# Eleven of 49 convolution taps on ScalarE and adding DMAs, and a folded layernorm inside fc1

## The chip, the cores and the metric

The kernel runs on one core of a Trainium2 chip. The metric is the device time of one execution in microseconds (us). The kernel before was timed three times: 3348.62, 3349.13 and 3350.71 us; the median is 3349.13. The profile is of one more execution, of 3348.34 us, whose span from the first to the last instruction is 3346.6 us. Engines are called as in the profile: PE (matmuls; PEld is its weight load), DVE (vector), ACT (scalar), POOL (GpSimd) and SP (the queue that issues most DMAs).

## The reference

Everything is float32. The input `x` has 8 images of 384 channels and 32 x 32 points. Two layers follow each other.

```python
# layer 0: attention block on 1024 tokens of 384 channels, per image
xn  = layernorm(xf, g1, beta1)
qkv = xn @ w_qkv.T + b_qkv                      # 8 heads of 48
out = softmax(q k^T * 48**-0.5) v
x1  = out @ w_proj.T + b_proj + xf
h   = gelu(layernorm(x1, g2, beta2) @ w_fc1.T + b_fc1)   # 384 -> 1536
x   = x1 + h @ w_fc2.T + b_fc2
# layer 1: convolution block
y   = depthwise_conv7x7(x, dw_w, padding=3) + dw_b
y   = layernorm(y over channels) * ln_w + ln_b
y   = gelu(y @ w1 + b1)                         # 384 -> 1536
y   = grn_gamma * (y * nx) + grn_beta + y       # nx from the norms of y over the image
x   = x + y @ w2 + b2
```

Each layernorm takes, for every token, the mean and the variance over the 384 channels.

## The kernel before

Channels lie on the 128 partitions, so an image is a tile of 128 x 3 x 1024; "half" h is a run of 512 tokens[...]. Both layers are done for one image after the other, and two images are in work at once: while PE does attention and mlp of image b, DVE does the 7 x 7 convolution of image b-1 and afterwards PE does the second layer of image b-1.

The program writes the order of every engine's work by hand. PE's matmuls are written in sequence; each helper that issues them tells `Flow.pe` how long they take (U = 0.857 us for one 128 x 128 by 512 product). Work of the other engines is written as generators, "chains": each yields the time after which its next step is due, and `Flow` takes that step as soon as the clock of PE's work has passed it. A chain spawned with `paced=True` counts its times from when a step was due, others from when it was taken. `flow.finish` issues all that is left of a chain at once. A due time only sets where an instruction stands in its engine's queue; what it has to wait for on the chip is set by semaphores. Every engine works its queue in order.

In the loop over images an iteration b from 1 to 6 runs: `qk` (queries and keys), `attention`, `mlp`, `keep` (the result goes to DRAM for later), `grn_up` of image b-1, `start_conv(b)`, `next_values(b+1)`, `grn_down` of image b-1. Image 7 has its own, `mlp_by_halves` and a convolution in pieces.

**Attention** has 64 steps; a step computes scores (four matmuls into a bank pair of `ps_s`, of which there are two), an exp of 128 x 1024 on ACT (`L601`), and two steps later the product with the values. When a head pair is complete, `average` divides by the softmax sums: a copy on ACT, an addition on DVE, and three short DMA hops on SP's queue. After step 38 `proj` of half 0 is put between, and ln2 of half 0 is spawned; `rest` does the second half, and is called inside fc1.

**mlp**: fc1 takes 12 tiles of half 0, with `rest` and ln2 of half 1 after the fourth, then 12 tiles of half 1, each with a Gelu on ACT. Then `before_fc2` is called, and fc2 follows as 15 products of a fast 3 x 3 x 2 scheme (`by_thirds`), with many additions on DVE and some as adding DMAs on POOL (`L786`). `grn_down` (w2) uses the same scheme.

**The convolution** (`convolution`, `L897`) has 49 taps for each of three channel tiles: one DVE instruction of 128 x 1024 each, the padded image times a column of weights plus the accumulator `acc`. Its paces `us` are 1.6 for image 0, 1.8 or 1.5 later, the first 30 instructions at 2.43. `next_norms`, called before fc2, finishes it.

**Layernorm** (`layernorm`): DVE adds the three channel tiles, a matmul with ones gives the sum over partitions (`token_sums`), DVE subtracts the mean, ACT squares, and the same is done for the variance; ACT makes the inverse root by Ln and Exp (which needs a table load[...]), and DVE multiplies. `token_sums` has a straight form, one 128 x 128 matmul for each half (`L374`), and a folded one: an adding DMA of POOL (`L382`) puts one half of the partitions on the other, 3.4 us are left for it, and 64 x 64 matmuls follow (`L388`), those of two halves in different quadrants of the array. `abreast` runs both halves side by side, with its times multiplied by a factor (1.4). ln1 and the first half of ln2 are folded; ln3, the convolution's layernorm, is not, and is spawned in `next_norms`, so it runs during fc2. `block_differences` prepares four combinations of its result.

`grn_scale` makes the factors of the second layer's norm and multiplies the 12 tiles of y by them on ACT (`L1074`). Tiles named "res" come from a ring of three.

Of the kernel before, what the change touches and what calls it, by code (L numbers as in the profile page):

```python
# [46 lines left out]
F32 = mybir.dt.float32  # L47
# [18 lines left out]
NC = HT // CM  # L66
U = 0.857
SCALE = HD ** -0.5
EPS0, EPS1, GRN_EPS = 1e-5, 1e-6, 1e-6
# [81 lines left out]
def block_kernel(  # L151
# [24 lines left out]
    ps_o = ctx.enter_context(tc.tile_pool(name="ps_o", bufs=4, space=PSUM))  # L176
    flow = Flow()
    s_fc2 = dram.tile([P, len(FORMS), 4 * P], F32, tag="s_fc2", bufs=1, name="s_fc2")
    s_w2 = dram.tile([P, len(FORMS), 4 * P], F32, tag="s_w2", bufs=1, name="s_w2")
# [186 lines left out]

    def token_sums(t, name, fold):

        width = t.shape[-1]
        if fold is None:
            total = o_tile(name)[:, :width]
            nc.tensor.matmul(out=total, lhsT=ones, rhs=t, start=True, stop=True)  # L374
            flow.pe(U * width / NH)
            return [(total, slice(0, width))]
        rows = [slice(0, 64), slice(64, P)]
        parts = [(fold, slice(0, width))]
        if fold == "columns":
            parts = [(j, slice(j * width // 2, (j + 1) * width // 2)) for j in range(2)]  # L380
        for j, cols in parts:
            nc.gpsimd.dma_start(out=t[rows[j], cols], in_=t[rows[1 - j], cols], accum_op=ALU.add)  # L382
        yield 3.4
        totals = []
        for j, cols in parts:
            total = o_tile(f"{name}_{j}")[:, : cols.stop - cols.start]
            for i in rows:
                nc.tensor.matmul(out=total[i, :], lhsT=ones[rows[j], :64], rhs=t[rows[j], cols], start=True, stop=True)  # L388
            flow.pe(U * width / NH / 2)
            totals.append((total, cols))  # L390
        return totals

    def layernorm(src, dst, h, eps, g, name, switch, spare=None, spaced=False, slow=1.0, fold=None, gentle=False):

# [15 lines left out]
        yield 2.6 * slow  # L410
        totals = yield from token_sums(a, f"{name}_sum{h}", fold)
        yield 0.8
# [18 lines left out]
        yield 1.8 * slow  # L431
        totals = yield from token_sums(squares[0], f"{name}_var{h}", fold)
        yield 0.8
# [21 lines left out]

    def abreast(*args, places=averages, fold=True, gentle=False, factor=1.4):

        chains = [
            layernorm(*args[:2], h, *args[2:], spare=places if h else None, fold=h if fold else None, gentle=gentle)
            for h in range(2)  # L460
        ]
        while chains:
            waits = []
            for chain in list(chains):
                wait = next(chain, None)
                if wait is None:
                    chains.remove(chain)
                else:
                    waits.append(wait)
            if waits:  # L470
                yield factor * max(waits)
# [109 lines left out]
    def attention(b, xt, qT, kT, last_tile, first):  # L581
# [44 lines left out]
        for n in range(len(steps) + 2):  # L626
# [4 lines left out]
            if n >= 2:  # L631
                product(*steps[n - 2], ps.pop(n - 2))
            if n - 2 == len(steps) // 2 + 6:
                for chain in first:
# [4 lines left out]
                proj(b, xt, 0)  # L639
                slow = 1.4 if b in (1, B - 1) else 1.0  # L640
                ln = layernorm(xt, xn, 0, eps0, "g2", f"ln2_{b}", False, spaced=True, slow=slow, fold="columns")
                ln = flow.spawn(ln)

        def rest():
            for m in (NP - 1, *range(CT)):
                flow.finish(chains[1, m])
            for seen, op in ((low, ALU.min), (high, ALU.max)):
                ext = small.tile([P, 1], F32, tag="ext", name=f"ext_{b}_{op.name}")
                nc.vector.tensor_reduce(ext, sums, AX.X, op)
                nc.vector.tensor_tensor(seen, seen, ext, op)  # L650
            proj(b, xt, 1)

        return ln, rest, xn
# [63 lines left out]

    def mlp(b, xt, xn, weights, tag, ln, rest, before_fc2):

# [4 lines left out]
        for m in range(HT):  # L724
            gelu_half(hid, m, 0, xn, weights, wa, f"fc1_{b}")
            if m == 3 and rest:
                rest()
                slow = 1.2 if b == 1 else 1.0
                ln = flow.spawn(layernorm(xt, xn, 1, eps0, "g2", f"ln2_{b}", True, slow=slow))
        flow.finish(ln)  # L730
        for m in range(HT):
# [147 lines left out]

    def convolution(acc, us, slow=0, y0=0, y1=H, ready=tuple(range(CT))):  # L880

# [3 lines left out]
        ct, n = None, 0  # L885
        while min(done) < KS * KS:
            left = [c for c in ready if done[c] < KS * KS]
            ct = min([c for c in left if c != ct] or left, key=lambda c: done[c])
# [10 lines left out]
            n += 1  # L899
            yield 2.43 if n <= CT * slow else us  # L900

    def block_differences(acc):
# [77 lines left out]
    def grn_down_straight(b, y, kept, weights, tag, index, todo):  # L980
# [5 lines left out]
        def load():  # L986
            if len(res) < len(todo):
                r, part = todo[len(res)]
                t = three.tile([P, NH], F32, tag="res", name=f"res_{b}_{r}_{part.start}")[:, : part.stop - part.start]
                nc.sync.dma_start(out=t, in_=kept[r * P : (r + 1) * P, part])  # L990
# [164 lines left out]
    def prepare(weights, aside):  # L1155
# [25 lines left out]
        def spare(name):  # L1181
            return three.tile([P, NH], F32, tag="res", name=name)

# [121 lines left out]
    def main():  # L1305
# [40 lines left out]

        state = {"xn": xn, "conv": None, "acc": None, "norm1": None, "norm3": None}
        kept = {}

        def start_conv(b, us, slow=0):  # L1350
            state["acc"] = one.tile([P, CT, N], F32, tag="acc", name=f"acc_{b}")
            state["conv"] = flow.spawn(convolution(state["acc"], us, slow), paced=True)

        def next_norms(b, ln=None):

            if b > 0:
                acc = state["acc"]
                flow.finish(state["conv"])
                norm = abreast(acc, acc, eps1, "lnw", f"ln3_{b - 1}", True, fold=False)
                norm = sequence(norm, block_differences(acc)) if b < B - 1 else after(ln, norm)  # L1360
                state["norm3"] = flow.spawn(norm)
            if b + 1 < B:
# [21 lines left out]
        def last_convolution(h, ct, ln=None):  # L1384
            if ct < 0:
                next_norms(B - 1, ln)
                return
# [8 lines left out]
        for b in range(B):  # L1396
# [6 lines left out]
            if b < B - 1:  # L1403
                mlp(b, xt, xn, weights, b, ln2, rest, lambda: next_norms(b))
            else:
# [5 lines left out]
            if b == 0:  # L1411
                xt = load_x(b + 1, "x")
                flow.finish(preparing)
                start_conv(b, 1.6)
                next_values(1)
# [4 lines left out]
            if b < B - 1:  # L1420
                y, gx = grn_up(b - 1, acc, weights, b - 1)
                start_conv(b, 1.5 if b == B - 2 else 1.8, 10)
                scale = flow.spawn(grn_scale(b - 1, gx, weights, b - 1, y))
                next_values(b + 1)
                flow.finish(scale)
                grn_down(b - 1, y, xt, weights, b - 1, b - 1)
                xt = load_x(b + 1, "x")
            else:
# [34 lines left out]
    def exact_path():  # L1463

        load_wqkv(nc.scalar, nc.scalar)
        with tc.For_i(0, B) as b:
# [10 lines left out]
            ln = layernorm(xt, xn, 1, eps0, "g2", "ln2_x", True)  # L1477
            mlp("x", xt, xn, weights, "x", ln, None, None)
            kept = keep("x", xt)
# [110 lines left out]
```

## Time and profile before

| what | value |
|---|---|
| span | 3346.6 us |
| PE busy | 3303.6 us, 99% |
| DVE busy | 2550.6 us, 76% |
| ACT busy | 1421.0 us, 42% |
| POOL busy | 208.1 us, 6% |
| convolution taps of 128 x 1024 on DVE | 1008 of 1276 ns |
| exps of attention on ACT | 512 of 1024 ns |
| images 2 to 6 | 404.2 us each |

Busy time is what an engine's own instructions take; matmuls overlap, so a record of 592 ns can start 429 ns after the one before it, and a float32 matmul has two records. A line such as `L382` is a line of the kernel, which may be that of a helper. In a group of the profile, `out<-in` names the tiles, "xN" counts, and what follows "idle before" is how long the engine stood still before these instructions, and who released it. PEclk is PE's granted clock.

### The profile page before, as it was taken

How to read it: one execution, taken by the hardware profiler on the slowest of the kernel's cores; microseconds unless marked ns; L12 is line 12 of the kernel's file. 1: busy time of each engine (PE TensorE's matmuls, PEld its weight loads, DVE VectorE, ACT ScalarE, POOL GpSimd, SP SyncE). 2: the span in 40 equal slices, each digit the busy share in tenths (PEclk: the TensorE clock that was granted, in tenths of full speed). 3: DMA queues.
4: the chain of work that ended last, by engine and by line, in shares of the span. 5: the costliest groups of instructions: out<-in, count | busy, mean ns of one | idle time of the engine just before them, and what ended most of it. 6: DMA issues, size and time to landing. Idle time of an engine off the chain costs nothing.

```text
span 3346.6 us, 37477 instructions
## 1 busy us (share of the span) xinstructions
PE 3303.6 (99%) x14282; PEld 1416.7 (42%) x14282; DVE 2550.6 (76%) x3133; ACT 1421.0 (42%) x1884; POOL 208.1 (6%) x243
## 2 busy tenths in 40 slices
PE   8999999999999999999999999999999999999999
PEld 4344434443344433444334443444434444334455
DVE  4344788887877878779797796967888779989950
ACT  3442453444534354352552625426254353522641
POOL 2121000100000000100001000010000110000000
PEclk9999999999999999999999999999999999999999
DMA  5336102642125410445005350062501633023231
GB/s 185 111 105 148 52 20 57 158 102 63 25 70 146 115 47 20 105 122 135 20 16 131 96 140 17 17 157 80 128 18 37 170 83 95 20 56 90 62 98 50
DMA packets 151243, 281.59 MB, mean 84 GB/s; under 512 B 35216, under 2 KB 41232, under 8 KB 150672
## 3 DMA queue, kind: packets, MB, share of 16 engines
q1 hardware_dynamic: 114704, 201.32, 19.6%
q0 software_dynamic: 36064, 77.08, 11.9%
q8 instruction: 115, 1.88, 0.2%
q10 hardware_dynamic: 288, 0.71, 0.1%
q14 instruction: 72, 0.59, 0.1%
HBM read 181.52 MB, written 33.82 MB: 64 GB/s over the span
## 4 chain that ended last, share of the span: by engine, by line
PE 87%; DVE 10%; DMA 2%; issue 1%; ACT 0%; SPq 0%; POOL 0%; DVEq 0%; POOLq 0%
PE o L612 12%; PE s L592 12%; PE fc L345 12%; PE h L352 10%; PE fc_p L352 10%; PE o_p L352 9%; PE qk L332 6%; DVE wqkv L897 4%; PE v L521 4%; PE o L1000 4%; PE proj L535 3%; DVE acc L897 3%; PE h_last L1044 1%; PE qk_last L345 1%; PE ln_var L374 1%
## 5 line engine op out<-in xcount | busy, mean ns | idle before, releaser
L897 DVE SCALAR_TENSOR_TENSOR acc<-pad,vec,acc 128x1024 f32<-128x1024 f32 x1008 | 1230.6, 1276 | 0.0
L601 ACT ACTIVATE p<-s 128x1024 f32<-128x1024 f32 x512 | 523.6, 1024 | 380.6 <-PE s L592 378.4
L592 PE MATMUL s<-qk 48*64 48x512 f32 x4096 | 544.0, 592 | 1.6 <-ACT qk L495 1.5
L612 PE MATMUL o<-p,v 64*64 64x512 f32 x4096 | 538.9, 590 | 0.0
L345 PE MATMUL fc<-xn,fc 128*128 128x512 f32 x1152 | 500.4, 593 | 0.0
L345 PEld LDWEIGHTS fc<-xn,fc 128*128 128x128 f32 x1152 | 218.2, 190 | 278.2 <-issue 268.2
L352 PE MATMUL fc_p<-hid,fc 128*128 128x512 f32 x728 | 318.1, 592 | 0.0
L364 ACT ACTIVATE hid<-fc,bfc_f 128x512 f32<-128x512 f32 x192 | 130.9, 687 | 357.5 <-PE fc L345 357.4
L612 PEld LDWEIGHTS o<-p,v 64*64 64x64 f32 x4096 | 158.6, 133 | 284.6 <-issue 278.1
L592 PEld LDWEIGHTS s<-qk 48*64 48x64 f32 x4096 | 155.5, 133 | 286.0 <-issue 264.3
L945 DVE TENSOR_TENSOR y<-h,y 128x512 f32<-128x512 f32 x288 | 197.2, 690 | 97.8 <-PE h L352 87.3
L352 PE MATMUL o_p<-y,w 128*128 128x512 f32 x624 | 270.9, 592 | 0.0
L352 PEld LDWEIGHTS fc_p<-hid,fc 128*128 128x128 f32 x728 | 138.2, 190 | 174.4 <-issue 170.4
L332 PE MATMUL qk<-xn,wqkv 128*128 128x512 f32 x480 | 207.4, 592 | 0.0
L352 PE MATMUL h<-acc,w_A 128*128 128x512 f32 x432 | 206.4, 596 | 0.0
L897 DVE SCALAR_TENSOR_TENSOR wqkv<-pad,vec,wqkv 128x416 f32<-128x416 f32 (+1 forms) x288 | 193.7, 749 | 0.6
L352 PEld LDWEIGHTS o_p<-y,w 128*128 128x128 f32 x624 | 118.0, 190 | 148.7 <-issue 133.5
L553 DVE TENSOR_TENSOR attn<-o,attn 128x512 f32<-128x512 f32 x64 | 44.1, 689 | 147.2 <-ACT attn L551 147.2
L495 ACT ACTIVATE qk<-qk,bqk 128x1024 f32<-128x1024 f32 x40 | 44.6, 1114 | 229.0 <-PE qk L332 229.0
L712 ACT COPY pad<-x 128x512 f32<-128x512 f32 x48 | 30.2, 635 | 258.3 <-DVE x L777 192.4
L332 PEld LDWEIGHTS qk<-xn,wqkv 128*128 128x128 f32 x480 | 91.1, 190 | 114.1 <-issue 112.0
L535 PE MATMUL proj<-attn,wproj_sb 128*128 128x512 f32 x288 | 129.2, 602 | 2.1 <-DVE attn L579 2.1
(296 smaller groups left out, 3342.5 us busy)
## 6 DMA issues: line engine op xcount, KB each, us to landing
w_A<-in_w SPq DMA_DIRECT2D x72, 384.0 KB, 3.2
fc<-s_fc SPq DMA_DIRECT2D x91, 256.0 KB, 2.8
hid<-hid POOLq DMA_DIRECT2D x42, 512.0 KB, 6.7
fc<-in_wfc SPq DMA_DIRECT2D x54, 384.0 KB, 5.7
w<-s_w SPq DMA_DIRECT2D x78, 256.0 KB, 2.7
y<-y POOLq DMA_DIRECT2D x36, 512.0 KB, 7.0
kept<-x SPq DMA_DIRECT2D x8, 1536.0 KB, 8.3
xn<-in_x SPq DMA_DIRECT2D x14, 768.0 KB, 7.0
```

What stands on the lines that cost most here:

```text
L332: nc.tensor.matmul(out=ps[:, half(h)], lhsT=lhsT(k), rhs=rhs(k)[:, half(h)], start=(k == 0), stop=(k == nk - 1),)
L345: nc.tensor.matmul(out=ps, lhsT=lhsT(k), rhs=rhs(k)[:, half(h)], start=(k == 0), stop=(k == nk - 1))
L352: nc.tensor.matmul(out=bank, lhsT=lhsT, rhs=rhs, start=k == 0, stop=k == len(pairs) - 1)
L364: nc.scalar.activation(dst, src, function, **kw)
L521: nc.tensor.matmul(out=ps[:, :C], lhsT=xn[:, k, t * P : (t + 1) * P], rhs=wv_sb[:, k, :], start=(k == 0), stop=(k == CT - 1),)
L535: nc.tensor.matmul(out=ps, lhsT=wproj_sb[:, m, ct * P : (ct + 1) * P], rhs=attn[:, m, :], start=(m == 0), stop=(m == CT - 1),)
L592: nc.tensor.matmul(out=s[64 * i : 64 * i + 64, j, :], lhsT=kT[64 * j : 64 * j + HD, m, k0 : k0 + 64], rhs=qT[64 * j : 64 * j + HD, m, half ...
L601: nc.scalar.activation(p, s, AF.Exp)
L612: nc.tensor.matmul(out=outs[i][64 * j : 64 * j + 64, :], lhsT=v[keys, t, at : at + 64], rhs=p[keys, j, :], start=(t == 0), stop=(t == KT - 1),
L897: nc.vector.scalar_tensor_tensor(dst, window, tap, dst, ALU.mult, ALU.add)
L945: nc.vector.tensor_tensor(dst, bank, part, ALU.add)
L1000: nc.tensor.matmul(out=ps, lhsT=tiles[k], rhs=y(k, part), start=(k == 0), stop=(k == HT - 1))
```

## The change

Three things are changed together.

The first is the taps. For images 0 to 6 the last eleven of the 49 taps of each channel tile are no longer DVE's. A new chain, `help_convolution`, takes the tiles one after the other, from the last. For each tap and half ACT multiplies 512 points of the padded image by the tap's weight into a "res" tile (the ring now has four), and a DMA of POOL adds that to `acc`; a tap is due every 2.1 us. While the chain holds a tile, and for 8 us after, the convolution leaves that tile out and works on the others. The list `quiet` holds the chain back: from two products before `proj` can begin until `proj` is issued, in both halves of attention, and throughout `grn_down`. The convolution's paces become 1.75 for image 0, and 2.0 with the first 24 instructions at 2.43 for the later ones.

The second is ln3. It now uses the folded sums and is spawned inside fc1, behind ln2's second half, by `conv_norm`; it waits for the convolution, its helper and that layernorm to be through. It leaves 5.0 us for a fold, times 1.4 (3.4 us times 2.4 for image 6's).

The third is ln2's first half, whose folds have 6.0 us instead of 3.4; two other factors of its times go from 1.4 to 1.2.

```diff
+HELPED = 11
+    quiet = []
-        yield 3.4
+        yield wait
...
+            if n - 2 in (len(steps) // 2 - 2, len(steps) - 2):
+                quiet.append("averages")
...
+                quiet.clear()
-                slow = 1.4 if b in (1, B - 1) else 1.0
-                ln = layernorm(xt, xn, 0, eps0, "g2", f"ln2_{b}", False, spaced=True, slow=slow, fold="columns")
+                slow = 1.2 if b in (1, B - 1) else 1.0
+                ln = layernorm(xt, xn, 0, eps0, "g2", f"ln2_{b}", False, spaced=True, slow=slow, fold="columns", wait=6.0)
...
                 ln = flow.spawn(layernorm(xt, xn, 1, eps0, "g2", f"ln2_{b}", True, slow=slow))
+                behind_ln(ln)
...
-        while min(done) < KS * KS:
-            left = [c for c in ready if done[c] < KS * KS]
+        taps = KS * KS - (HELPED if taken is not None else 0)
+        while min(done) < taps:
+            left = [c for c in ready if done[c] < taps and not (taken and taken.get(c, 0) > flow.now)]
+            if not left:
+                yield 1.0
+                continue
...
+    def help_convolution(acc, us, taken):
+        yield 8.0
+        for ct in reversed(range(CT)):
+            taken[ct] = float("inf")
+            for i in range(KS * KS - HELPED, KS * KS):
+                dy, dx = divmod(i, KS)
+                for h in range(2):
+                    while quiet:
+                        yield 1.0
+                    t = three.tile([P, NH], F32, tag="res", bufs=4, name=f"tap_{ct}_{i}_{h}")
+                    y0 = dy + h * H // 2
+                    window = pad[:, ct, y0 : y0 + H // 2, dx : dx + W]
+                    tap = col("dww", ct * KS * KS + i)
+                    nc.scalar.mul(t.rearrange("p (h w) -> p h w", w=W), window, tap)
+                    nc.gpsimd.dma_start(out=acc[:, ct, half(h)], in_=t, accum_op=ALU.add)
+                    yield us
+            taken[ct] = flow.now + 8.0
+        yield 8.0
+        taken.clear()
...
+            state["conv"] = flow.spawn(convolution(acc, us, slow, taken=taken), paced=True)
+            state["help"] = flow.spawn(help_convolution(acc, 2.1, taken), paced=True)
-        def next_norms(b, ln=None):
+        def conv_norm(b, ln):
             if b > 0:
                 acc = state["acc"]
-                flow.finish(state["conv"])
-                norm = abreast(acc, acc, eps1, "lnw", f"ln3_{b - 1}", True, fold=False)
-                norm = sequence(norm, block_differences(acc)) if b < B - 1 else after(ln, norm)
-                state["norm3"] = flow.spawn(norm)
+                how = dict(wait=5.0) if b < B - 1 else dict(wait=3.4, factor=2.4)
+                norm = abreast(acc, acc, eps1, "lnw", f"ln3_{b - 1}", True, **how)
+                if b < B - 1:
+                    norm = sequence(norm, block_differences(acc))
+                state["norm3"] = flow.spawn(after(ln, after(state["help"], after(state["conv"], norm))))
+        def next_norms(b):
+            if b > 0:
+                flow.finish(state["help"])
+                flow.finish(state["conv"])
...
-                start_conv(b, 1.6)
+                start_conv(b, 1.75)
...
-                start_conv(b, 1.5 if b == B - 2 else 1.8, 10)
+                start_conv(b, 2.0, 8)
...
+                quiet.append("w2")
                 grn_down(b - 1, y, xt, weights, b - 1, b - 1)
+                quiet.clear()
```

## The prediction

> **What bounds the kernel now.** I read first the page's busy table, then the busy times cut at the image boundaries, then PE's own list of waits, and last the groups that the change touches.
>
> ```profile
> PE 3303.6 (99%) x14282; PEld 1416.7 (42%) x14282; DVE 2550.6 (76%) x3133; ACT 1421.0 (42%) x1884; POOL 208.1 (6%) x243
> ...
> q0 software_dynamic: 36064, 77.08, 11.9%
> ```
>
> A busy PE need not be at its peak, so the share alone proves nothing. The table by image settles it (stretch; its length, then busy time of PE, PEld, DVE, ACT, POOL; clock; DMA share):
>
> ```profile
> 334.65:760.90 426.25, 422.14 (x1791) 178.62 (x1791) 353.91 (x402) 182.37 (x232) 23.29 (x22) 1.00 0.31 79
> ...
> 1165.17:1569.43 404.26, 403.89 (x1743) 169.26 (x1743) 326.08 (x378) 178.25 (x222) 23.35 (x22) 1.00 0.33 82
> ...
> 2377.84:2782.04 404.20, 403.83 (x1744) 169.03 (x1743) 326.00 (x378) 178.25 (x222) 23.34 (x22) 1.00 0.32 83
> 2782.04:3156.00 373.96, 362.96 (x1622) 149.31 (x1621) 344.15 (x450) 151.91 (x189) 3.34 (x4) 0.99 0.20 55
> ```
>
> Images 2 to 6 take 404.2 us each, the same to 0.07 us, although DVE is free for 78 of them. A 512-column f32 matmul starts 0.857 us after the one before (two records 0.429 apart); an image holds about 467 such units, 400 us. So only some 4 us per image are not streaming, and taking work off DVE is worth nothing there unless PE waits for DVE. Where it waits (total us, times, longest):
>
> ```profile
> PE ln_sum L374 <- DVE ln_a L409: 12.9, 5, 6.3
> PE ln_var L374 <- DVE ln_sq L430: 8.7, 8, 5.9
> ...
> PE ln_var L388 <- DMA ln_sq<-ln_sq: 2.2, 3, 1.2
> PE proj L535 <- DVE attn L579: 2.1, 1, 2.1
> ```
>
> By PE's timeline the first two lines are mostly the start-up (10 us) and image 7; the last two are image 1 and image 7. The steady images hardly appear.
>
> **What the Trainium skill says, and what the trace says to it.** "ScalarE: Activation LUTs", What ACT_TABLE_LOAD costs: an ACTIVATE takes 186 ns + 0.833 ns per element, 93 ns more for a pointer operand, and neighbours overlap by 93. The trace agrees: `L707` (immediate, 1024 elements) 1048 ns, `L1074` (column scale) 1137. A tap of 512 with a column scale is thus priced at 706 ns, 0.62 net. "DMA: Bandwidth & Descriptors", Anatomy of one DMA: about 2.0 us + bytes/436e3. For an accumulate of 512 KB that is 3.2 us; the trace has 5.2 to 9.4 (below), so I use the trace. Same page, Queues, rings and completion order: each DMA engine takes turns between queue rows, packet by packet, so taps slow loads rather than stand behind them; the trace of before has no taps to show it. "TensorE: Matmul & The Clock Gate", Part 1: after an idle window PE runs at half rate for some 3.4 us. The trace agrees: after the 2.08 us wait at 517.5 seven proj records took 4.97 us, where 3.2 is normal. A wait of 2 us or more costs nearly twice itself.
>
> **The change, part by part**, against the profiled span of 3346.6 us (its own run 3348.3; the three timed ones have the median 3349.1, so I add 2.5 at the end).
>
> *1. Folded sums of ln3, seven images (b-1 = 0 to 6).* PE's timeline of before has both forms: unfolded in fc2, folded for ln1 in the up projection.
>
> ```profile
> 1392.06 1.02 PE L374 MATMUL ln_sum<-ln_a,ones 128*128 128x512 f32 x2
> 1392.92 1.02 PE L374 MATMUL ln_sum<-attn,ones 128*128 128x512 f32 x2
> 1393.78 2.74 PE L352 MATMUL fc_p<-hid,fc 128*128 128x512 f32 x6
> ...
> 1449.66 0.65 PE L388 MATMUL ln_sum<-ln_a,ones 64*64 64x512 f32 x2
> ...
> 1450.74 1.12 PE L352 MATMUL h<-acc,w_A 128*128 128x512 f32 x2
> ```
>
> Unfolded: 1393.78 - 1392.06 = 1.72 us for both halves. Folded: four 64x64 quadrants run abreast, 1450.74 - 1449.66 = 1.08, plus 0.09 before: 1.17. Saved 0.55 per sum, two sums, seven images: 7.7 us. The four fold DMAs per image have 5.0 x 1.4 = 7.0 us (8.2 in image 7) until their matmuls; `ln<-ln` of this size landed in 4.7. POOL's fc_e DMAs (1369.3, 1374.5 in image 2) may stand before the second pair: still inside 7.0. Cost 0; bound 1 us per image.
>
> *2. ln3 moved from fc2 into fc1.* It issues per image 4 fold DMAs on POOL (new), 20 DVE instructions and the 4 of `block_differences`, 6 squares, 4 Ln/Exp and a table load on ACT, and forces one more Gelu table load: about 2 x 1.28 + 6 x 0.6 + 4 x 0.6 = 8.6 us of ACT. The stretch 1350 to 1388 has ACT busy for 12.35 of 38 us and DVE, then without taps, free; PE's banks turn over four deep at 2.57 us. Cost 0.
>
> *3. 66 taps per image on ACT and POOL, 33 fewer on DVE.* DVE loses 33 x 1.24 = 41 us per image: worth nothing in images 2 to 6. ACT gains 66 x 0.62 = 41 us. Attention is the tight place: 1193 to 1250 had ACT busy 35.2 of 57 us; a tap every 2.1 us adds 27 x 0.62 = 16.8, so 52 of 57. A score bank has 2.57 us from its matmuls to its reuse, exp takes 1.02, so one tap before an exp fits (1.55 left). Bounds 0 to 2 us per image; taken 0.2. Before the w2 products four taps pass: the scaling `L1074` is just in time there, but ACT idles 0.4 us between each copy of v and the next, which takes 0.53 of the tap: about 0.1 late; taken 0.1.
>
> DMA: q0's share gives 0.119 x 16 x 3346.6 / 36064 = 0.177 us per packet, mostly 2 KB; a tap has 128 rows, so 128 x 0.177 / 16 = 1.4 us of all engines every 2.1 us, 0.67. Attention has 0.10 before, qk 0.38; qk is overfull for some 10 us, but what it loads (x, fc1's weights) is wanted 100 us later. SP's short DMAs (sums, back, r, about 2 us each) get slower beside taps; DVE waits for them in order, with 78 + 41 us to spare. The helper pauses in w2, where the share is 0.64, and for the averages.
>
> New waits: on POOL a tap's DMA waits for ACT's product and for DVE's last tap on that tile; behind it stand ln2's folds (item 4). On DVE the first tap on a tile given back waits for the landing; it is issued 10.1 us (2.1 + 8) after the last tap DMA, so it finds it landed; behind it would stand the averages and ln2's sums.
>
> *4. ln2's fold allowance 3.4 to 6.0.* Its two DMAs queue on POOL behind up to two taps (1 us each to issue, 1.4 to move); 2.7 us become 5 to 7. The longer chain (5.2 us) has 45 us before fc1. The sums can make PE wait for up to 1 us, twice: taken 0.3 per image (0 to 2).
>
> So 3 and 4 cost about 0.6 per image, 7 images: 4 us.
>
> *5. Image 1.* It takes 426.25 - 404.2 - 15.5 (values at the boundary) = 6.5 us too long, with DVE 100% busy in its attention (1.22 at ln_var, 2.08 at proj and the slow clock after it). Taps at 1.75 instead of 1.6 us, averages undisturbed: the cause goes. Taken 5 of 6.5 (0 to 6.5).
>
> *6. Image 7.* The convolution of image 6 now ends at about 2715 + 24 x 2.43 + 90 x 2.0 = 2953, and not in a burst behind 2961. The waits of 1.0 + 0.4 at 2913 and 2.43 at 2966 go: 4 us. The 5.92 at 3007 goes too (factor 2.4), but from 2990 to 3109 DVE never rests (last convolution), so PE would meet it later, where it now waits 1.4 at 3110. Taken 4 (0 to 12).
>
> Sum: -7.7 - 5 - 4 + 4 = -12.7. Span 3333.9, runs 3336.
>
> **The rivals.**
> *The saving is eaten (about 3347, -2).* Items 3 and 4 near their ends, 1.8 us per image, 12.6 in all, and item 5 only half. For it: exp's slack in attention falls from 0.70 to nearly nothing. Against: ACT still sums to 0.91 and the order gives 2.57 us.
>
> *Tap buffers block ACT (slower, about 3390).* A tap takes one of four "res" buffers, so ACT waits when a tap has not landed 4 x 2.1 = 8.4 us after its start; exp stands behind it on ACT, and PE behind exp. ACT's remaining idle, about 9 us per attention, covers up to 9 us of landing; at 9.5 it is (9.5/4 - 2.1) x 62 = 17 us per image less 9, times 7 = 56: 3392. Evidence:
>
> ```profile
> DMA to landing us min/median/max: 5.2/6.8/9.4
> ```
>
> These are the 512 KB accumulates at DMA share 0.7; a tap is half of that, so 5 us and 1 to 2 before it: under 8.4. It decides from 9 us on.
>
> *All of it comes (about 3322).* Image 7 gives 12 instead of 4, image 1 6.5, no new waits: -7.7 - 6.5 - 12 = -26.
>
> That the change does not act is excluded for the folds (the form runs already); for the taps it is items 3 and 5.
>
> **How the numbers follow.** Main case 0.50 (3330 to 3342), all of it 0.12, eaten 0.21, blocked 0.17. About 0.2% (6.7 us) can be told from no change, so faster is 0.50 + 0.12 = 0.62, same 0.21, slower 0.17. Range 3325 to 3356: it leaves out half of the fourth case at the bottom and most of the blocked one at the top.
>
> **What would show each step.** Images 2 to 6 at 403 to 404 us; `ln3` sums as 64*64 groups of 1.1 us; tap ACTIVATEs at 0.71 us, tap DMAs landing at 4 to 6 us; no PE wait named after "tap" or exp in attention; image 1 near 420 us with its boundary; the 2.43 at 2966 gone and a longer wait near 3105. Wrong if ACT's waits on tap DMAs are long, if images take 405 us or more, or if ln2's sums wait for their DMA by over 1 us.

## The result, and the profile after

The changed kernel takes 3378.3 us (median of 4 runs, 3374.4 to 3385.0) where the kernel before takes 3349.4: ratio 1.0088, 95% interval 1.0069 to 1.0107. It is slower by 29 us; 3336 was predicted, with 3356 as the upper end. The profiled execution has a span of 3372.7 us, 26.1 more than before, and all sums below are made against these two spans. One execution each of the kernel before (8371.6 us) and of before_rest_later (4998.2 us) was in a slow state and is left out of the ratios below.

The page's busy table and its busiest queue, of the changed kernel (us, share of the span, instructions; packets, MB, share of the DMA engines):

```profile
PE 3310.5 (98%) x14338; PEld 1415.1 (42%) x14338; DVE 2284.8 (68%) x2902; ACT 1688.4 (50%) x2348; POOL 623.4 (18%) x733
...
q0 software_dynamic: 104832, 201.90, 33.5%
```

The work went where it was sent: DVE has 266 us less, ACT 267 more, and the queue of the taps carries 125 MB more. PE is busy for only 7 us more, so the loss is mostly in PE's gaps. Images 2 and 3 of the changed kernel, cut where `qk` begins (length, busy times of PE, PEld, DVE, ACT and POOL, clock, DMA share, GB/s):

```profile
757.30:1169.70 412.40, 405.36 (x1752) 168.00 (x1751) 288.06 (x345) 215.75 (x288) 82.71 (x92) 1.00 0.57 124
1169.70:1579.60 409.90, 405.44 (x1752) 168.06 (x1751) 288.19 (x345) 215.84 (x288) 82.75 (x92) 1.00 0.58 125
```

404.2 us became 412.4 and 409.9, and the length is no longer the same from image to image, which speaks for waits that depend on the moment and against a fixed price. PE's list of waits (total, times, longest):

```profile
PE proj L539 <- DVE attn L583: 17.7, 6, 4.9
PE ln_sum L376 <- DVE ln_a L412: 11.0, 6, 6.1
PE s L596 <- ACT p L605: 8.1, 13, 1.8
PE h L334 <- ACT h L1010: 4.9, 1, 4.9
```

The second line was there before (12.9). The first has grown from 2.1; the third and fourth are new. A wait costs more than itself, because PE's next records can come more slowly (shown at `proj` below). To weigh the waits with these slow stretches, I took for each stretch of PE's records the time from start to start less 0.857 us for each product of 512 columns; call it the excess (slightly negative where products overlap better than that). Summed over images 1 to 7:

| excess, us | before | after | difference |
|---|---|---|---|
| at `proj` | 7.8 | 30.7 | +22.9 |
| at the scores in attention | -1.0 | 14.1 | +15.0 |
| all else, with the shorter sums | | | -11.8 |
| span | 3346.6 | 3372.7 | +26.1 |

The third row is the remainder. So the two new waits cost 38 us, and what else the change does gave back about 12. That this is close to the predicted sum of 12.7 is chance: the gains alone (items 1, 5 and 6) were summed to 16.7, and 12.7 is what was left of them after 4 us of costs.

**The wait at proj.** DVE's timeline about the end of attention, image 3, of the kernel before. The last two averages are an addition (`L553`) and a multiply (`L579`) each:

```profile
1304.80 0.69 DVE L553 TENSOR_TENSOR attn<-o,attn 128x512 f32<-128x512 f32 x1 [0.37 <-ACT attn L551]
...
1313.30 0.69 DVE L579 TENSOR_TENSOR attn<-attn,r 128x512 f32<-128x512 f32 x1 [1.76 <-DMA r<-back]
...
1316.69 0.69 DVE L553 TENSOR_TENSOR attn<-o,attn 128x512 f32<-128x512 f32 x1 [0.32 <-ACT attn L551]
...
1326.00 0.69 DVE L579 TENSOR_TENSOR attn<-attn,r 128x512 f32<-128x512 f32 x1 [1.70 <-DMA r<-back]
```

and the same work in the changed kernel, whose attention ends at 1323.2 and not at 1316.0:

```profile
1312.23 2.07 DVE L447 SCALAR_TENSOR_TENSOR xn<-xn,vec,ln_rstd 128x512 f32<-128x512 f32 x3
1314.22 0.69 DVE L557 TENSOR_TENSOR attn<-o,attn 128x512 f32<-128x512 f32 x1
...
1326.17 0.69 DVE L583 TENSOR_TENSOR attn<-attn,r 128x512 f32<-128x512 f32 x1 [5.88 <-DMA r<-back]
...
1329.17 0.68 DVE L557 TENSOR_TENSOR attn<-o,attn 128x512 f32<-128x512 f32 x1
...
1337.69 0.69 DVE L583 TENSOR_TENSOR attn<-attn,r 128x512 f32<-128x512 f32 x1 [2.69 <-DMA r<-back]
```

PE in the same place:

```profile
1333.54 1.88 PE L539 MATMUL proj<-attn,wproj_sb 128*128 128x512 f32 x4
1338.44 7.97 PE L539 MATMUL proj<-attn,wproj_sb 128*128 128x512 f32 x14 [3.02 <-DVE attn L583]
```

The times that follow count from the end of attention. The first addition started at -11.2 us and now starts at -9.0, directly behind ln2's multiply (`L447`). The first multiply came at -2.7 and comes at +3.0. DVE stands 5.88 us in front of it, because a hop of the average (`r<-back`) has not landed, and the last average's addition, which could have run at about 0.7, is queued behind it and starts at +6.0. So the last multiply moves from +10.0 to +14.5. `proj` reaches its first matmul at +10.3 and needs that tile two products later. It stands for 3.02 us, and from there to the next fc1 product in PE's timeline its 14 records take 1346.25 - 1338.44 = 7.81 us instead of 14 x 0.429 = 6.0.

So the first multiply is 5.7 us late for two reasons: its addition starts 2.2 us later, and the way from it to the multiply, three hops and a reciprocal, takes 12.0 us instead of 8.5. Over images 2 to 6 the first shift is 2.0 to 2.7 us; without the tap DMAs (products_only, below) it is still 1.5 to 1.7. The time from addition to multiply was 8.4 to 9.3 us and is 9.7 to 12.0; in products_only it is 8.4 to 8.7, in one image 10.3. The lengthening therefore goes with the DMAs, and most of the first shift does not.

DVE's idle time in front of all 48 multiplies (us, times) in the kernel before, and then in the changed one:

```profile
  DMA r<-back: 76.3, 39
```

```profile
  DMA r<-back: 166.5, 48
```

The hop of 32 KB itself, before and after (count, KB each, median us from issue to landing):

```profile
r<-back SPq DMA_DIRECT2D x96, 32.0 KB, 2.0
```

```profile
r<-back SPq DMA_DIRECT2D x96, 32.0 KB, 3.0
```

**The wait at the scores.** ACT beside `qk` of image 3:

```profile
1191.25 0.72 ACT L929 ACTIVATE tap<-pad,vec 128x512 f32<-128x512 f32 x1 [3.76 <-DMA acc<-tap]
```

and POOL, which issues what ACT has made:

```profile
1191.73 0.85 POOL L930 DMA_DIRECT2D acc<-tap  x1 [6.85 <-DMA acc<-tap]
```

Within a channel tile, a tap's DMA adds to the same half of `acc` as the one two before it, and the program makes it wait until that one has landed. So two are in flight at a time, save where the tile changes: 13 of the 462 were issued with two earlier ones still under way. Where a landing takes long, POOL stands (6.85 us here), the four buffers fill, ACT is held, and the bias and exp instructions behind the tap come late. In the attention that follows, ACT is held again, and the exp behind that tap lets PE wait:

```profile
1208.40 0.72 ACT L929 ACTIVATE tap<-pad,vec 128x512 f32<-128x512 f32 x1 [1.30 <-DMA acc<-tap]
1209.03 1.01 ACT L605 ACTIVATE p<-s 128x1024 f32<-128x1024 f32 x1
```

```profile
1210.09 1.09 PE L596 MATMUL s<-qk 48*64 48x512 f32 x8 [0.98 <-ACT p L605]
```

The answer on the line of the tap DMAs gives the sums (us, times; then the landing):

```profile
  DMA acc<-tap: 260.2, 148
...
  ACT tap L929: 67.0, 52
...
DMA to landing us min/median/max: 3.2/3.5/9.9
```

The first of these is how long POOL sat until an earlier tap had landed, the second how long ACT was held.

### The profile page after: what moved, and what is told of

It reads as the page before. It is cut to its first block, busy times and chain, and to the rows that moved or that the text cites. A ratio compares the mean times of both kernels' runs of the same rounds, so it can differ in the third digit from the quotient of the medians.

```text
span 3372.7 us, 38961 instructions
## 1 busy us (share of the span) xinstructions
PE 3310.5 (98%) x14338; PEld 1415.1 (42%) x14338; DVE 2284.8 (68%) x2902; ACT 1688.4 (50%) x2348; POOL 623.4 (18%) x733
## 4 chain that ended last, share of the span: by engine, by line
PE 78%; DMA 8%; DVE 7%; issue 3%; ACT 2%; SPq 2%; POOL 0%; DVEq 0%; ACTq 0%; POOLq 0%
PE fc L347 12%; PE fc_p L354 10%; PE h L354 10%; PE s L596 9%; PE o L616 9%; PE o_p L354 8%; DMA acc<-tap 4%; PE v L525 4%; PE o L1034 4%; PE qk L334 4%; PE proj L539 3%; DVE wqkv L910 3%; DVE acc L910 2%; DMA r<-back 2%; PE h_last L1078 1%
## 5 line engine op out<-in xcount | busy, mean ns | idle before, releaser
L910 DVE SCALAR_TENSOR_TENSOR acc<-pad,vec,acc 128x1024 f32<-128x1024 f32 x777 | 958.5, 1276 | 2.4
L930 POOL DMA_DIRECT2D acc<-tap x462 | 395.8, 875 | 1171.0 <-ACT tap L929 493.3
L929 ACT ACTIVATE tap<-pad,vec 128x512 f32<-128x512 f32 x462 | 334.2, 730 | 67.9 <-DMA acc<-tap 67.0
L720 ACT COPY pad<-x 128x512 f32<-128x512 f32 x48 | 30.2, 635 | 261.4 <-DVE x L786 194.5
L539 PE MATMUL proj<-attn,wproj_sb 128*128 128x512 f32 x288 | 136.4, 626 | 17.8 <-DVE attn L583 17.7
```

The costliest lines, as they stand in the source:

```text
L539: nc.tensor.matmul(out=ps, lhsT=wproj_sb[:, m, ct * P : (ct + 1) * P], rhs=attn[:, m, :], start=(m == 0), stop=(m == CT - 1),)
L910: nc.vector.scalar_tensor_tensor(dst, window, tap, dst, ALU.mult, ALU.add)
L929: nc.scalar.mul(t.rearrange("p (h w) -> p h w", w=W), window, tap)
L930: nc.gpsimd.dma_start(out=acc[:, ct, half(h)], in_=t, accum_op=ALU.add)
```

## The experiments

Each ran beside the kernel before on the same chip (its medians there: 3346.4 to 3350.1). Excess in us over images 1 to 7; the last column is image 7 with the end. An excess is that of the one profiled execution, not of the median: adds_only's profiled execution took 3373.5 us, 13 above its median, the others' lie within 4 us of theirs. So differences of a few us between excesses of two kernels are not to be trusted.

| kernel | median us | ratio, 95% interval | proj | scores | image 7 |
|---|---|---|---|---|---|
| before | 3349.4 | | 7.8 | -1.0 | 20.5 |
| after | 3378.3 | 1.0088, 1.0069 to 1.0107 | 30.7 | 14.1 | 19.7 |
| products_only | 3339.2 | 0.998, 0.9969 to 0.999 | 6.6 | 1.3 | 20.0 |
| adds_only | 3360.4 | 1.0045, 1.0031 to 1.0058 | 44.5 | -1.1 | 20.7 |
| fold_only | 3362.8 | 1.005, 1.0037 to 1.0064 | 4.8 | -1.0 | 22.1 |
| no_help | 3366.2 | 1.0056, 1.0041 to 1.0071 | 14.5 | -1.0 | 28.4 |
| rest_later | 3353.0 | 1.0015, 1.0008 to 1.0022 | 3.8 | 14.4 | 23.2 |
| five_buffers | 3372.5 | 1.0066, 1.005 to 1.0083 | 39.9 | 1.1 | 21.9 |
| early_quiet | 3373.3 | 1.0075, 1.0058 to 1.0092 | 19.0 | 12.2 | 33.6 |
| quiet_qk | 3374.9 | 1.0078, 1.0061 to 1.0095 | 32.6 | 9.9 | 23.1 |
| both | 3341.1 | 0.9974, 0.9963 to 0.9986 | 6.5 | 1.4 | 23.1 |
| both_unfolded | 3350.5 | 1.001, 1.0001 to 1.0019 | 8.4 | 3.9 | 17.7 |
| before_rest_later | 3348.4 | 1.0000, 0.9991 to 1.0009 | 4.2 | 0.7 | 22.6 |
| short_ln2 | 3380.1 | 1.0097, 1.008 to 1.0114 | 19.5 | 13.2 | 30.2 |

**ACT's products without the DMAs.**

```diff
-                    nc.gpsimd.dma_start(out=acc[:, ct, half(h)], in_=t, accum_op=ALU.add)
```

> The changed kernel without the adding DMAs of the taps: ACT still makes all 462 products, nothing is added (those eleven taps are left out of the result). Theory A (the DMAs' landing is what hurts: ACT held by its four buffers, and the short DMAs of the averages slowed): excess at the scores and at proj goes, images of 403 to 404 us, about 3338 us. Rival (ACT's own 0.62 us per tap makes exp and the averages' copy late): proj still waits 2 us or more per image and the time stays above 3360.

3339.2 us, images of 403.1 to 405.3. Theory A held: the 462 products on ACT cost little at the scores (2.3 us of excess more than before, over seven images) and nothing in sum at proj (6.6 against 7.8). This kernel leaves out what the eleven taps add, so its time is a measurement and not an alternative.

**The DMAs without ACT's products.**

```diff
-                    nc.scalar.mul(t.rearrange("p (h w) -> p h w", w=W), window, tap)
+                    t = wproj_sb.rearrange("p c o -> p (c o)")[:, h * NH : (h + 1) * NH]
```

> The changed kernel with the tap DMAs but without the ACT products: each DMA adds a constant piece of the projection weights instead (so those eleven taps are wrong in the result). Theory A: ACT is never held, so the scores do not wait, but the averages' DMAs still take 4 us and proj waits some 3 us per image: about 3355 to 3365 us. Rival (it takes both, a late copy on ACT and slow DMAs): little of the proj wait is left, under 3348.

3360.4 us. The proj wait is there in full. In PE's waits of this kernel it is larger than in the changed one, but they are of an execution of 3373.5 us, so how much larger it is in the median stays open:

```profile
PE proj L539 <- DVE attn L583: 23.8, 6, 4.4
```

The wait at the scores is gone, since no ACT instruction waits for a buffer. With the run above this is the division: the DMAs make the proj wait with no products on ACT; the scores' wait needs DMAs and products together.

**The fold alone, in fc2.**

```diff
-                norm = abreast(acc, acc, eps1, "lnw", f"ln3_{b - 1}", True, fold=False)
+                norm = abreast(acc, acc, eps1, "lnw", f"ln3_{b - 1}", True, fold=True)
```

> The kernel before with one word changed: ln3 stays in fc2 but uses the folded sums (allowance 3.4 x 1.4 = 4.8 us). Theory A (the fold saves 0.55 us per sum, the taps cost all the rest): 14 sums, 7.7 us less, 3341 to 3343 us. Rival (the fold itself brings waits, since its DMAs stand among the adding DMAs of fc2, which moved at a share of 0.72): each of 14 sums waits 1 us or more, 3350 us or above, with PE waits at the folded sums named after a DMA.

3362.8 us; theory A was wrong and the rival right. Steady images take 406.6 us (one 407.4): in fc2 the excess per image at ln_var grows from 0.45 to 2.4 and at `fc_p` from nothing to 2.3, more than the sums save. PE's waits of this kernel:

```profile
PE ln_var L388 <- DMA ln_sq<-ln_sq: 8.0, 8, 1.2
...
PE fc_p L352 <- issue: 4.6, 5, 1.1
```

What holds `fc_p` the profile does not name.

**No taps given away, ln3 folded inside fc1.**

```diff
-            state["conv"] = flow.spawn(convolution(acc, us, slow, taken=taken), paced=True)
-            state["help"] = flow.spawn(help_convolution(acc, 2.1, taken), paced=True)
+            state["conv"] = flow.spawn(convolution(acc, us, slow), paced=True)
```

(and the paces 1.6 for image 0 and 1.65 later, so that 49 taps are done in time)

> The changed kernel with all 49 taps on DVE again (paces 1.65, for image 0 1.6), the fold and ln3's place inside fc1 kept. Theory A (taps cost the rest): images 2 to 6 at 403 us, no proj wait but in image 1, about 3338 to 3345 us. Rival (moving ln3 into fc1, with the convolution then pressed into less time, costs): images of 406 us and more with DVE full in attention, 3355 us or above.

3366.2 us; theory A was wrong here too. With 41 us more on DVE in each image, images take 405.6 to 409.4, and image 7 pays most:

```profile
PE proj L539 <- DVE attn L583: 7.8, 5, 3.2
PE fc L347 <- DVE xn L419: 5.6, 1, 5.6
```

So relief of DVE, which I had called worth nothing in images 2 to 6, has a worth: it makes room for ln3 in fc1. Slower and faster paces were not tried, so a part of the loss may be the pace's.

**Rest's proj two fc1 tiles later.**

```diff
-            if m == 3 and rest:
+            if m == 5 and rest:
```

> The changed kernel with rest and ln2's second half behind the sixth tile of fc1 instead of the fourth: 5.1 us more of PE work ahead of proj. Theory A: the late average is covered, proj waits in image 5 alone (8.1 before), images 405 to 406 us, about 3356 us, unless ln2's second half then comes late for fc1's second half (some 1 us). Rival (the delay grows with the room, since the helper and the averages move too): proj still waits 2 us or more, 3370.

3353.0 us (20 runs), 25 less than the change. DVE still sits 166.5 us in front of the multiplies, as much as in the changed kernel, and PE no longer waits for them. From this kernel's answer on that line:

```profile
  DMA r<-back: 166.5, 48
```

The lateness of the averages is unchanged; 5.2 us of other work in front of proj (it comes at +15.5 instead of +10.3) covers it. The scores' wait stays, as expected.

**A fifth buffer.**

```diff
-                    t = three.tile([P, NH], F32, tag="res", bufs=4, name=f"tap_{ct}_{i}_{h}")
+                    t = three.tile([P, NH], F32, tag="res", bufs=5, name=f"tap_{ct}_{i}_{h}")
```

(and so at the two other uses of the ring)

> The changed kernel with five res buffers instead of four; nothing else. Theory A (ACT is held because a tap holds its buffer over 8.4 us, each tap DMA waiting for the one two before it on the same half of acc): 10.5 us are allowed, the scores' excess falls from 15 us in all to about 5, proj stays as it is, about 3368 us. Rival (the scores wait since ACT is simply full): no change, 3375 to 3380.

The scores' excess falls to 0.1 in images 2 to 6, and ACT's hold with it; ACT's waits of this kernel (67.0, 52 in the changed one):

```profile
ACT tap L929 <- DMA acc<-tap: 10.6, 13, 1.3
```

The median falls by only 6 us. In the profiled execution (3375.5 us, 3 above the median) proj's excess is 9 us larger than in the changed kernel; why, and whether it is so in the other executions, stays open.

**Taps held back for longer before the end of attention.**

```diff
-            if n - 2 in (len(steps) // 2 - 2, len(steps) - 2):
+            if n - 2 in (len(steps) // 2 - 2, len(steps) - 10):
```

> The changed kernel, the helper held back eight attention steps (13.7 us) earlier before the end of attention, so that the last two averages have no taps beside them; its remaining taps move behind rest. Theory A (tap DMAs lengthen the DMA hops of the last but one average, DVE waits for it in order and does the last average late): the proj excess falls from 2 to 8 us per image to 1 or less, about 20 us in all, 3355 to 3362 us; the excess at the scores stays. Rival (the last average itself is slow for another reason, as DVE's load): proj unchanged, 3375 us or more.

A partial miss: proj's excess falls from 30.7 to 19.0 and not to the level before, and the taps pushed back are paid for in image 7 (excess 33.6; PE waits there 8.3 us for DVE's `xn`). The time from the first addition to its multiply is back at 8.4 to 8.6 us in three of images 2 to 6, but that addition still starts late (-7.4 to -8.5 us). Taps near the last averages are part of the cause, not all.

**Taps held back during qk.**

```diff
-HELPED = 11
+HELPED = 8
```

(the later images' pace 1.9, and `quiet` kept from `grn_down` through the next image's `qk`)

> The changed kernel with the helper held back through qk as well, and eight helped taps per tile instead of eleven so that it still ends in time (DVE pace 1.9). Theory A (the x load of qk is what puts the tap DMAs behind, 8.5 to 9.6 us there, and attention begins with that backlog): the scores' excess goes to 0 or below 0.5 us per image, 15 us less; proj still waits, 3360 to 3366 us. Rival (serial landing alone, with 3.3 us each, holds ACT in attention): the scores still wait 1 us or more per image.

The scores' excess stays at 1.4 to 1.8 us in images 1 to 6 (0.7 to 4.9 in the changed kernel), which is the rival's number; but the trace does not show its cause. ACT is held before taps 9 times, for 17 us (52 times, 67 us in the changed kernel), and all nine lie between 356 and 389 us, in image 1, whose qk has no `grn_down` before it and so no `quiet`. In images 2 to 7 ACT is never held, and the wait at the start of attention is gone, as theory A said. What remains lies elsewhere. In image 3, ACT has taps, the squares of ln2, the copy of an average and exps one behind the other, and an exp comes late:

```profile
1297.68 0.75 ACT L929 ACTIVATE tap<-pad,vec 128x512 f32<-128x512 f32 x1
1298.33 1.93 ACT L605 ACTIVATE p<-s 128x1024 f32<-128x1024 f32 x2
```

```profile
1299.40 1.09 PE L596 MATMUL s<-qk 48*64 48x512 f32 x8 [0.59 <-ACT p L605]
```

So the hold of the changed kernel begins with the taps beside qk's loads, and a schedule in which taps meet ln2's squares has a wait of its own. The edit also takes three taps per tile off ACT, and their part was not told apart.

**Both remedies.** The edits of rest_later and of five_buffers together.

> The changed kernel with rest behind the sixth fc1 tile and five res buffers. Theory A (the two waits are all that the taps cost): images of 403 to 404 us, no excess at scores and proj, 3336 to 3342 us, faster than before by 0.2% or a little more. Rival (ACT, now never held, starts taps sooner, so more tap DMAs stand beside the averages and folds, and proj or ln2's sums wait again): images of 405 us or more, 3346 or above.

3341.1 us (7 runs, 3336.1 to 3343.5): 0.9974 of the kernel before, and so faster than either kernel. Images 2 to 6 take 403.1 to 404.5; both waits are gone.

**Both, with ln3's sums unfolded.**

```diff
-                norm = abreast(acc, acc, eps1, "lnw", f"ln3_{b - 1}", True, **how)
+                norm = abreast(acc, acc, eps1, "lnw", f"ln3_{b - 1}", True, fold=False, **how)
```

> The kernel of both with ln3's sums straight again, in its place inside fc1. Theory A (the fold saves 0.55 us per sum and its adding DMAs are hidden there): 14 x 0.55 = 7.7 us more than both. Rival (the fold's gain is eaten by slots of its quadrants or by waits for its DMAs): the same as both to 2 us.

3350.5 us, 9.4 us more than both; 7.7 was my sum for the fold. Not all of the difference is the fold: the profiled execution has 7 us more at proj and the scores in images 5 and 6, and 5 us less in image 7. A clean image, the second, takes 404.1 against 403.2. The kernel before took 3349.2 us beside it: with both waits removed and no fold, eleven taps less on DVE and ln3's new place make the kernel no faster. They only make room for the fold.

**Rest's place, alone.** The edit of rest_later in the kernel before.

> The kernel before with rest behind the sixth fc1 tile, nothing else. Theory A: its steady images do not wait at proj, so only image 1 gains (4 us of its proj wait): 3343 to 3346 us. Rival (the later ln2 second half comes too late for fc1's second half, or fc2 gets crowded): 3350 us or above.

1.0000 of the kernel before: proj's wait in image 1 goes (4.6 to 0.5), its fc1 and attention take 3.2 us more. So what rest_later gains is the change's own loss undone, and what both gains does not come from rest's new place.

**ln2's folds as before.**

```diff
-                ln = layernorm(xt, xn, 0, eps0, "g2", f"ln2_{b}", False, spaced=True, slow=slow, fold="columns", wait=6.0)
+                ln = layernorm(xt, xn, 0, eps0, "g2", f"ln2_{b}", False, spaced=True, slow=slow, fold="columns")
```

> The changed kernel with the folds of ln2's first half given 3.4 us again instead of 6.0; nothing else. In the trace of the changed kernel ln2's multiply of three instructions on DVE (2.07 us) stands 11 us before the end of attention, directly ahead of the addition of the last average but one; before, it stood 19 us ahead of that end. Theory A: the adding DMAs alone make rest's proj wait, through late landings of r; then proj's excess over the even stream stays where it is (30.7 us over images 1 to 7 in the changed kernel, 7.7 in the one before), within 5 us, and the time stays within 5 us of 3378. Rival: ln2's later place on DVE is a good part of the cause; then that addition starts at 10 us or more before the end of attention instead of 8.5 to 9.0, its multiply about 2 us sooner, proj's excess falls by 8 us or more, and the time to 3370 or less. Either way the sums of ln2's first half may now wait for their fold DMA, up to 1 us each.

Each theory was right in one half. The time stays (3380.1), as A said; but proj's excess falls by 11.2, as the rival said, and the averages move as it said: the addition at -11.1 to -11.3 us in images 4 to 7, -9.4 and -9.6 in images 2 and 3. What is won is lost in the sums, which now wait for their fold DMAs. PE's waits of this kernel:

```profile
PE proj L539 <- DVE attn L583: 9.8, 6, 2.7
PE ln_var L390 <- DMA ln_sq<-ln_sq: 5.0, 5, 2.4
...
PE ln_sum L390 <- DMA ln_a<-ln_a: 3.1, 2, 2.2
```

The excess of the sums ln_sum and ln_var, over images 1 to 7, rises from 4.8 to 17.8. Image 7's excess rises by 10.5 us, in part through these sums.

## Why the prediction was wrong

*Item 3, the DMA side: the step that failed.* "SP's short DMAs get slower beside taps; DVE waits for them in order, with 78 + 41 us to spare." The first two clauses came true: the 32 KB hop of r has a median of 3.0 us instead of 2.0, and up to 5.3 in the average looked at in images 2 to 6. The error is the last clause. Free time of DVE over an image is no slack for a chain of hops with a due time. The slack that mattered could have been read from the trace before: the last multiply at +8.7 to +10.0 us, rest's proj at +10.3. The multiply takes 0.7 us and its tile is wanted two products (1.7 us) after proj's start, which leaves 1.3 to 2.6 us, and not 119. Two averages share one DVE queue, so the second inherits the first's delay. This step was taken at 0 and measured +22.9 us.

That it needs the DMAs is shown by adds_only and products_only; that it costs only through proj's place, by rest_later. The DMAs are not alone. With ln2's multiply in its late place and no DMAs, proj's excess is 6.6 us (products_only); with the DMAs and ln2's folds as before, 19.5 (short_ln2); with both, 30.7; with neither, 7.8. So the late place costs nothing by itself and about half of the loss together with the DMAs. Holding the taps back earlier also removes about half (early_quiet); these two overlap, and I did not run them together.

*Item 3, the taps' buffers: mis-sized.* "5 us and 1 to 2 before it: under 8.4." The median landing is 3.5 us, better than the 5 that I took. But I left out that the DMA itself waits on POOL for the one two before it, so a buffer's time is the wait, the issue and the landing: of the DMA issued at 1191.73 the issue alone came 6.85 us after POOL's last. Taken 0.2 us per image, measured 15.0 us over seven, 2.1 each. The rival "tap buffers block ACT" had the right mechanism and the right side, with a price of 56 us and a limit on the landing alone, both wrong: the sum of the three counts. five_buffers shows it. That its 3390 is nearer to the result than 3336 is in good part luck, since 23 of the 38 us of waits are proj's. In quiet_qk, with no taps beside qk's loads, the hold of images 2 to 7 is gone, which points to the slow landings there as its start.

*Item 3, prices: right.* A tap on ACT takes 0.73 us (0.71 predicted); the load itself is harmless (products_only).

*Items 1 and 2: right in the changed kernel, and tied to each other.* Predicted were 0.55 us per sum, 1.1 per image; clean images are 1.1 us shorter (403.1 in both and products_only, 404.2 before), and both against both_unfolded gives 9.4 us, with the reservation above. The sums hardly wait there (excess about -0.16 at ln_sum and ln_var in most images). But fold_only and no_help show that neither fc2 nor an fc1 with all taps on DVE has room for the fold; I had charged DVE's relief with no worth.

*Item 4: too small.* Taken 0.3 per image for the sums; those don't wait with 6.0 us. What the later ln2 does to the averages beside the tap DMAs was not in the sum: about 11 us (30.7 against 19.5 in short_ln2).

*Item 5: failed.* Image 1 was to gain 5 us beside the fold's 1.1; it gained 2.8 in all (410.7 to 407.9). Its proj excess stays at 4.8 (4.6 before); what goes is the 2.9 at ln_var. In place of the busy DVE that I had named there are now late hops in front of proj; for image 1 alone this was not tested.

*Item 6: failed in its size, right in its shape.* ln_var's excess in image 7 falls from 10.8 to 4.6, and the wait is met later, at `h`, for ACT: from 0.3 to 6.4. Gain 0.8 instead of 4. The 4.9 us wait for ACT stands in every kernel with ln3 folded in fc1 and not in both_unfolded; what delays ACT there was not tested.

*The signs that I had named* were good ones: images at 405 us or more, a PE wait named after exp, long waits of ACT on tap DMAs were all to show me wrong, and all came; PE's waits for the DMA of a folded sum, a fourth sign, stayed under 1 us. The sign that I had missed is a wait of proj on DVE with `r<-back` behind it.

With both waits removed the kernel runs in 3341.1 us, 8 less than the kernel before, where 12.7 had been summed. What is missing is mainly in image 7, which was to gain and has an excess of 23.1 us against 20.5 before.

## What to carry to other kernels

Before work is put beside a chain of short DMAs, measure that chain's slack at its consumer: when does the last of it end, and when is it wanted. The free share of the engine that it passes through (119 us per image here) did not show that 1.3 to 2.6 us were all there was. For adding DMAs into one tile, count how many may be in flight: here each waits for the last that touched the same bytes, and the buffer that feeds it is held for that wait too.

## What the runs showed of the hardware

An adding DMA of 256 KB within SBUF lands after 3.2 us at best, 3.5 in the median and 9.9 at worst. With two destinations used in turn and each DMA waiting for the last on its own, POOL stood 260 us for landings. The trace is consistent with the Trainium skill, "DMA: Bandwidth & Descriptors", Queues, rings and completion order, where each DMA engine takes turns between the queues that have work: beside the taps of one queue the median 32 KB hop on another took 3.0 us instead of 2.0 (2.3 in adds_only), still less than the 3.5 that a tap takes to land. The turns themselves no run shows. DVE's own taps took the same time beside POOL's 462 DMA issues as before (mean 1276 ns in both profiles).

After a wait PE's records came up to 0.853 us apart instead of 0.429: 1.8 us were lost after the 3.02 us wait of image 3 in the changed kernel, and 1.8 after the 2.08 us wait at 517.5 in the kernel before. The granted clock of image 3 is 1.00 in the table by images and does not show this. The page that the prediction names for it, "TensorE: Matmul & The Clock Gate" of the Trainium skill, Part 1, gives an idle window of about 3.4 us as what slows PE; here a slow stretch followed a wait of 2.08 us already, and the measurement decides.
